# Splitting the transformed 3x3 convolution's matmuls into four column-tiled ones

## The chip, the cores and the metric

The kernel runs on one core of a Trainium2 chip. The metric is the device time of one execution in microseconds, the median of the runs shown. A core has TensorE (PE in the profile, with its weight loads as PEld), VectorE (DVE), ScalarE (ACT), GpSimd (POOL) and SyncE (SP), which here issues most of the DMAs. Matmul results land in PSUM; everything else that is worked on lies in SBUF.

## The reference

The input x has 8 images of 512 channels by 32 x 32 pixels, all float32. Two residual layers follow each other. Only the first one holds the code of this change.

```
x = x + L0(group_norm(x))
    t = silu(bn(conv1x1(x)));  ys = [t[:, :256], t[:, 256:]]
    for i in range(2):
        yi = ys[-1]
        z = silu(bn(conv3x3(yi, m_cv1_w[i])))      # 256 -> 256 channels   <- changed here
        z = attention(z, qkv_w[i], rw[i] + rh[i])   # 4 heads of 64, 1024 positions
        z = silu(bn(conv1x1(z, m_cv2_w[i])))
        ys.append(yi + z)
    silu(bn(conv1x1(concat(ys), cv2_w)))
x = x + L1(group_norm(x))
    depthwise 3x3, bn, relu, prune; conv1x1, bn, relu, prune
```

## The kernel before

The images are worked on one after the other, with channels on the 128 partitions and the 1024 pixels along the free dimension. The order of all work is written out by hand. Each piece of work is registered under a short name (`add("P", ...)`), and strings of names (`FIRST`, `HEAD`, `TAIL`, `LAST`) say in which order the pieces are issued: `P` is a call of `products`, `d` a step of the input transform, `Rc` and `R` the two steps that take a result back out of PSUM, `B`, `E` and `Ez` the rest of the back transform, `s`, `e`, `p` and `w` the steps of attention. A class `InOrder` (L95) ties every engine's instructions to that order; since it issues all of them, every line of the profile carries L105, and groups are told apart by the tiles that they write and read.

The 3x3 convolutions don't multiply pixel by pixel. `conv3` (L725) transforms the input rows along x (`along_rows`) and along y (`across_rows`) on VectorE into three pairs of planes j, each in one tile: `comps` (L741) names `kr`, `vt` and `qy`, which are free at this point, for j = 0, 1, 2. A tile holds four components c of 512 columns. In a component, 128 columns belong to each pair of output half i and input block k, in the order 2 * i + k. The weights were transformed in the same way at the start and stored in DRAM (`u_dram`); each call of `products` takes one tile of them, 128 x 2048, from a ring of five (`ring`, profile name `wring`), and `ring_load` fetches the next.

`products(j, m)` (L791) makes for one pair of planes j and one block m of 128 output channels all the products of transformed weights and transformed input: for each of four components c and two halves i, two matmuls of 128 input channels by 128 output channels by 128 columns, which add up over k in the same place of a PSUM tile. That tile, `ps_c3` (`ps_c` in the profile), is 128 x 1024 and comes from a pool of two, `ps_big`, that attention and the 1x1 convolutions use too. `rows_back` (L810) then copies one component to SBUF on ScalarE and adds and subtracts the four on VectorE into `mid`. The six calls of one convolution follow each other on TensorE with no other matmul between them; 8 images, 2 layers and 6 calls make 96 calls of 16 products each.

Attention holds the two halves of the array apart already: scores (`ps_s`) and values (`ps_av`) work on quarters, 64 rows by 64 columns. The sums of the softmax (`sums`, L1030, tile `ps_dn`) use 128 rows and 32 columns, four tiles side by side:

```python
for i in range(4):
    t = sm[m, i // 2]
    nc.tensor.matmul(
        dn[32 * i : 32 * (i + 1), :], ones, t[:, i % 2, :], start=True, stop=True
    )
```

Of the kernel before, what the change touches and what calls it, by code (L numbers as in the profile page):

```python
# [15 lines left out]
P = 128  # L16
# [4 lines left out]
HEADS, HD = 4, 64  # L21
# [104 lines left out]
def fast_kernel(  # L126
# [16 lines left out]
    nc = Engines(tc)  # L143
# [18 lines left out]
    def big_tile(name):  # L162
        return ps_big.tile([P, 2, 512], F32, tag="big", name=name)
# [121 lines left out]
    def flat(ps):  # L285
        return ps.rearrange("p n f -> p (n f)")
# [126 lines left out]
    def ring_load(n=1):  # L413
        for _ in range(n):
            if not sources:
                continue
            if holds and len(sources) <= holds[0]:
                waiting[0] += 1
                continue
            src = sources.pop(0)  # L420
            t = ringp.tile([P, 2048], F32, tag="ring", name="wring")
            o = t[:, : src[1]]
            if src[1] == 1024:
                o = o.rearrange("p (k o) -> p k o", o=P)
            nc.sync.dma_start(o, src[0])
            ring.append(t)
# [298 lines left out]
    def conv3(l):  # L725
# [17 lines left out]
        def component(j, c):  # L743
            return comps[j][:, c * 512 : (c + 1) * 512]
# [46 lines left out]
        def products(j, m):  # L791

            ps = banks[j, m] = big_tile("ps_c3")
            u = ring.pop(0).rearrange("p (i c k o) -> p i c k o", i=2, c=4, k=2)
            for c in (1, 2, 0, 3):
                for i in range(2):
                    at = place[c] * 256 + i * P
                    for k in range(2):
                        nc.tensor.matmul(
                            flat(ps)[:, at : at + P],  # L800
                            u[:, i, c, k, :],
                            component(j, c)[:, (2 * i + k) * P : (2 * i + k + 1) * P],
                            start=(k == 0),
                            stop=(k == 1),
                        )
            ring_load()

        inner_planes, outer_planes, ys = {}, {}, {}
# [60 lines left out]
        for j in range(3):  # L869
            add("d", *[lambda j=j, i=i: along_rows(j, i) for i in range(2)])  # L870
            add("d", *[lambda j=j, i=i: across_rows(j, i) for i in range(2)])
        add("P", *[lambda j=j, m=m: products(j, m) for j, m in jm])
        add("Rc", *[lambda j=j, m=m: rows_back(j, m, 0) for j, m in jm])
        add("R", *[lambda j=j, m=m: rows_back(j, m, 1) for j, m in jm])
# [1000 lines left out]
```

## Time and profile before

| | |
|---|---|
| time, median of 2 runs | 2595.19 us (2595.06 to 2595.32) |
| span of the profiled execution | 2593.6 us |
| around the span, against the median | 1.6 us |
| mean granted TensorE clock | 0.997 |
| instructions | 36377, of them 14806 matmuls and as many weight loads |
| PE, DVE, ACT busy | 2557.7, 2054.9, 1214.4 us |
| ps_c matmuls | 3 groups (kr, vt, qy) of 1024, 119.4, 117.0 and 117.0 us |

The page gives the busy time of each engine, then the span in 40 slices, the DMA queues, the chain of work that ended last, and the costliest groups of instructions. A row of a group reads: line, engine, operation, output<-inputs, rows*columns of the array for a matmul, shape, count, then busy time in us, mean ns of one instruction, and the idle time ahead of it with what ended it. The duration of a single matmul reaches from its start to the modelled end of its pass through the array, so that it is longer than the distance between two; the distance is busy time or elapsed time divided by the count. Rows of the order of time read: start in us, length in us, engine, operation, count.

### The profile page before, as it was taken

What the parts mean: (1) busy time and instruction counts of PE and PEld (TensorE: products, weight loads), DVE (VectorE), ACT (ScalarE), POOL (GpSimd) and SP (SyncE); (2) the same over time, 40 slices, a digit from 0 to 9 for tenths busy, and PEclk for the clock granted to TensorE, in tenths of its full rate; (3) what the DMA queues carried; (4) which work ended last, traced back from release to release, by engine and by line L of the source; (5) the groups of instructions that cost most, each with busy time, mean ns of one, the idle gap of its engine ahead of it and who ended that gap; (6) DMA issues with size and microseconds to landing.
All of it is one profiled execution on the core that took longest, in us unless ns stands there. A gap on an engine that the chain in (4) does not pass through costs nothing.

```text
span 2593.6 us, 36377 instructions
## 1 busy us (share of the span) xinstructions
PE 2557.7 (99%) x14806; PEld 1292.0 (50%) x14806; DVE 2054.9 (79%) x2954; ACT 1214.4 (47%) x1551; POOL 129.2 (5%) x99
## 2 busy tenths in 40 slices
PE   8999999999999999999999999999999999999997
PEld 5454463634636346463464635545355544645443
DVE  8887588877897877877778778787788877888657
ACT  3635446353463544635445444544445454363534
POOL 1000000000100000000000000000001000010000
PEclk9999999999999999999999999999999999999998
DMA  9445230522305214060140702306122151312300
GB/s 347 157 155 203 66 122 25 167 98 73 113 27 199 66 65 122 17 247 18 65 122 17 248 18 81 105 24 241 33 96 75 61 204 34 130 45 82 122 17 34
DMA packets 83791, 268.51 MB, mean 104 GB/s; under 512 B 7072, under 2 KB 37536, under 8 KB 69408
## 3 DMA queue, kind: packets, MB, share of 16 engines
q1 hardware_dynamic: 76032, 248.01, 27.2%
q0 software_dynamic: 4032, 14.68, 3.1%
q10 hardware_dynamic: 3552, 3.41, 0.4%
q8 instruction: 118, 1.93, 0.3%
q14 instruction: 57, 0.47, 0.1%
HBM read 212.34 MB, written 36.96 MB: 96 GB/s over the span
## 4 chain that ended last, share of the span: by engine, by line
PE 95%; DVE 3%; ACT 1%; issue 0%; DMA 0%; SPq 0%; DVEq 0%; ACTq 0%
PE ps_av L105 16%; PE ps_s L105 16%; PE ps_c L105 13%; PE ps_cv L105 12%; PE ps_qk L105 8%; PE ps_cv2q L105 8%; PE ps_q L105 7%; PE ps_v L105 4%; PE ps_y L105 4%; PE ps_m L105 4%; PE ps_dn L105 1%; ACT qy L105 1%; DVE sum L105 1%; DVE ht L105 1%; PE ps_pw L105 0%
## 5 line engine op out<-in xcount | busy, mean ns | idle before, releaser
L105 ACT ACTIVATE e<-ps_s 128x1024 f32<-128x1024 f32 x512 | 509.7, 1023 | 286.8 <-PE ps_s L105 265.6
L105 PE MATMUL ps_s<-qy,kr 64*64 64x512 f32 x4096 | 513.7, 592 | 1.4
L105 DVE TENSOR_TENSOR sum<-sum,e 128x1024 f32<-128x1024 f32 x384 | 475.2, 1238 | 39.2 <-ACT e L105 19.9
L105 PE MATMUL ps_av<-e,vt 64*64 64x512 f32 x4096 | 506.2, 590 | 0.0
L105 DVE SCALAR_TENSOR_TENSOR ht<-xn,v_sb,ht 128x961 f32<-128x961 f32 (+1 forms) x256 | 317.3, 1247 | 8.6 <-ACT ht L105 5.0
L105 PEld LDWEIGHTS ps_s<-qy,kr 64*64 64x64 f32 x4096 | 160.5, 132 | 289.0 <-issue 191.1
L105 PEld LDWEIGHTS ps_av<-e,vt 64*64 64x64 f32 x4096 | 165.4, 133 | 277.4 <-issue 266.0
L105 PE MATMUL ps_qk<-z,wring 128*128 128x512 f32 x512 | 231.1, 596 | 2.0 <-ACT z L105 1.3
L105 DVE TENSOR_TENSOR sum<-e 128x1024 f32<-128x1024 f32 x64 | 78.1, 1220 | 164.0 <-ACT e L105 162.6
L105 ACT COPY c<-ps_c 128x256 f32<-128x256 f32 x96 | 35.6, 371 | 259.4 <-PE ps_c L105 259.3
L105 PEld LDWEIGHTS ps_qk<-z,wring 128*128 128x128 f32 x512 | 95.6, 190 | 115.7 <-issue 101.5
L105 DVE RECIPROCAL r<-ps_dn 128x128 f32<-128x128 f32 x128 | 113.7, 925 | 11.2 <-PE ps_dn L105 9.0
L105 PE MATMUL ps_c<-vt,wring 128*128 128x128 f32 x1024 | 119.4, 276 | 2.3 <-DVE v L105 1.3
L105 PEld LDWEIGHTS ps_c<-kr,wring 128*128 128x128 f32 x1024 | 116.8, 192 | 8.0 <-issue 6.1
L105 PEld LDWEIGHTS ps_c<-vt,wring 128*128 128x128 f32 x1024 | 116.2, 192 | 4.3 <-ACT c L105 2.3
L105 PE MATMUL ps_c<-qy,wring 128*128 128x128 f32 x1024 | 117.0, 275 | 0.0
L105 PE MATMUL ps_c<-kr,wring 128*128 128x128 f32 x1024 | 117.0, 275 | 0.0
L105 PE MATMUL ps_cv<-pt,w_sb 128*128 128x512 f32 x256 | 116.7, 607 | 0.0
L105 PE MATMUL ps_v<-wring,z 128*128 128x256 f32 x512 | 115.9, 379 | 0.7 <-DVE kr L105 0.7
L105 PEld LDWEIGHTS ps_c<-qy,wring 128*128 128x128 f32 x1024 | 115.6, 192 | 0.0
L105 PE MATMUL ps_m<-z,wm_sb 128*128 128x512 f32 x256 | 112.5, 592 | 0.0
L105 PE MATMUL ps_y<-pt,w_sb 128*128 128x512 f32 x256 | 112.3, 592 | 0.0
(178 smaller groups left out, 3255.5 us busy)
## 6 DMA issues: line engine op xcount, KB each, us to landing
wring<-u SPq DMA_DIRECT2D x96, 1024.0 KB, 4.8
pt<-in_x SPq DMA_DIRECT2D x32, 512.0 KB, 9.4
rw<-r SPq DMA_DIRECT2D x64, 256.0 KB, 3.4
xt<-in_x SPq DMA_DIRECT2D x32, 512.0 KB, 7.5
out<-xt SPq DMA_DIRECT2D x32, 512.0 KB, 8.0
kr<-r POOLq DMA_DIRECT2D x28, 512.0 KB, 6.6
wring<-q SPq DMA_DIRECT2D x14, 896.0 KB, 4.6
wring<-in_wqkv SPq DMA_DIRECT2D x16, 768.0 KB, 4.4
```

Source lines behind the costliest of these rows:

```text
L105: made = method(*args, **kwargs)
```

## The change

The two halves of the 128 columns (n) are multiplied separately, and for each the two halves of the 128 output channels (o). `HD` is 64. Each matmul has still 128 rows, but 64 columns of weights and 64 moving columns, and it writes one half of the PSUM partitions, by which it sits on the left or on the right half of the array's columns. The sums over k are finished for the first half of the columns before the second is begun. Everything else stays.

```diff
             for c in (1, 2, 0, 3):
                 for i in range(2):
                     at = place[c] * 256 + i * P
-                    for k in range(2):
-                        nc.tensor.matmul(
-                            flat(ps)[:, at : at + P],
-                            u[:, i, c, k, :],
-                            component(j, c)[:, (2 * i + k) * P : (2 * i + k + 1) * P],
-                            start=(k == 0),
-                            stop=(k == 1),
-                        )
+                    for n in (0, HD):
+                        for k in range(2):
+                            from_ = (2 * i + k) * P + n
+                            for o in (0, HD):
+                                nc.tensor.matmul(
+                                    flat(ps)[o : o + HD, at + n : at + n + HD],
+                                    u[:, i, c, k, o : o + HD],
+                                    component(j, c)[:, from_ : from_ + HD],
+                                    start=(k == 0),
+                                    stop=(k == 1),
+                                )
             ring_load()
```

## The prediction

> **What bounds the kernel now.** I read the page's shares of busy time first, then the chain that ended last, then the groups of instructions, then the order of time around one convolution and one attention stage.
>
> ```profile
> PE 2557.7 (99%) x14806; PEld 1292.0 (50%) x14806; DVE 2054.9 (79%) x2954; ACT 1214.4 (47%) x1551; POOL 129.2 (5%) x99
> ...
> PE 95%; DVE 3%; ACT 1%; issue 0%; DMA 0%; SPq 0%; DVEq 0%; ACTq 0%
> ...
> L105 PE MATMUL ps_c<-vt,wring 128*128 128x128 f32 x1024 | 119.4, 276 | 2.3 <-DVE v L105 1.3
> L105 PEld LDWEIGHTS ps_c<-kr,wring 128*128 128x128 f32 x1024 | 116.8, 192 | 8.0 <-issue 6.1
> ```
>
> TensorE is busy for 99% of the span and holds 95% of the chain. Whatever lengthens a matmul stage lengthens the program; there is no large wait in which it could hide. The three ps_c matmul groups (kr, vt, qy) are what the change touches: 3 x 1024 records. Each product in the code leaves two loads and two matmuls in the trace (two passes), so these are 1536 products: 96 calls of `products` (8 images, 2 layers, 3 components, 2 output blocks), each with 16.
>
> The longest pieces of the chain, in order of time, then the window of the same piece (columns of the last line: stretch, its length, then busy time of PE, PEld, DVE, ACT, POOL, clock, DMA share, GB/s):
>
> ```profile
> 347.58 21.44 PE ps_c L105 x192
> ...
> 347.58:369.02 21.44, 21.44 (x193) 21.44 (x193) 20.46 (x46) 3.77 (x11) 0.00 (x0) 1.00 0.61 209
> ```
>
> Here six calls follow one another without a gap: 21.44 us / 192 matmuls = 111.7 ns each, and 3072 x 111.7 = 343.1 us, 13% of the span, which is the share that the chain gives ps_c. In this stretch the loads (PEld) are busy all the time too, unlike over the whole span (50%). So each step of 111.7 ns is bounded by both: 128 moving columns stream while the next 128 columns of weights load.
>
> How column tiles behave is shown by a stage that has them already, ps_dn (128 rows by 32 columns, four tiles), between two attention stages of 64 by 64 tiles:
>
> ```profile
> 120.66 1.04 PE L105 MATMUL ps_av<-e,vt 64*64 64x512 f32 x8
> 121.63 1.07 PE L105 MATMUL ps_dn<-sum,ones 128*32 128x512 f32 x8
> 122.63 1.09 PE L105 MATMUL ps_s<-qy,kr 64*64 64x512 f32 x8
> 123.54 1.04 PE L105 MATMUL ps_av<-e,vt 64*64 64x512 f32 x8
> ...
> 121.63 0.16 PEld L105 LDWEIGHTS ps_dn<-sum,ones 128*32 128x32 f32 x8 [0.81 <-issue]
> ...
> L105 PEld LDWEIGHTS ps_dn<-sum,ones x256: 106/108/110, 121.6 to 2479.7; 128*32 128x32 f32 x128
> L105 PEld LDWEIGHTS ps_s<-qy,kr x4096: 129/133/133, 89.2 to 2476.1; 64*64 64x64 f32 x196
> L105 PEld LDWEIGHTS ps_c<-kr,wring x1024: 186/192/192, 43.3 to 2383.6; 128*128 128x128 f32 x171
> ```
>
> To be seen: (1) eight ps_dn matmuls of 512 columns take 1.07 us, where eight in a row would take 8 x 0.43 = 3.4 us (a full-array 512-column matmul, ps_qk, costs 231.1 us / 512 = 0.45). So four column tiles of the same 128 rows run at once, in two rounds of 0.43 us. (2) Their eight loads are all done within 0.16 us: the loads of different column tiles run at once, and the second four run beneath the first four matmuls. (3) A load's median falls from 192 to 133 to 108 ns for 128, 64 and 32 columns, 0.75 to 0.92 ns a column on a fixed part. (4) A normal eight of this kind begins every 0.86 us; the ps_dn eight was late by 0.11 us, and ps_s came 1.00 us after it: a switch of tile shape costs something.
>
> [...] No group here shows a stream of 64-column matmuls.
>
> **The change, part by part.** Each product (128 input rows, 128 outputs, 128 columns, 2 passes of load and matmul) becomes four: two halves of the moving columns (n) by two halves of the outputs (o), on the left and right half of the array. The k loop now lies inside n, and o innermost, so neighbours in the program sit on different halves. Removed: 3072 loads of 128 columns and 3072 matmuls of 128. Added: 12,288 loads of 64 columns and 12,288 matmuls of 64. Multiplications are the same; loaded weight columns double in total, but two halves can load at once. No DMA, VectorE, ScalarE instruction or buffer is changed, and the waits on ring tile, component and psum tile stay at each call's start.
>
> *Step of one pair of tiles.* With both halves at once, a round is a left and a right matmul. In the trace's single starts, matmuls of 512 and 256 columns follow at 428.8 and 215.8 ns, 0.83 ns a column[...]. So the old step is 128 x 0.833 = 106.7 ns plus 5.0 fixed = 111.7. With the same fixed part, a step of 64 columns is an estimated 53.3 + 5.0 = 58.3 ns. Four rounds (n twice, passes twice) replace two steps: 4 x 58.3 = 233.2 against 2 x 111.7 = 223.4 ns, +9.8 ns a product; 1536 of them: +15.0 us. The gain from halves is exactly eaten by the doubled count, and what remains is the fixed part paid twice.
>
> Nothing in before shows this step, so I bound it. Below: streaming, 53.3 ns, plus the smaller fixed part of the 512-column steps (428.8 - 512 x 0.833 = 2.2): 55.5 ns, -1.4 ns a product, -2 us. Above: the halves do not overlap at all, 8 x 58.3 = 466 ns, +243 ns a product, +373 us. I take 58.3, as ps_dn shows the overlap.
>
> *Instructions.* A round now hands over 4 instructions in 58 ns, where it was 2 in 112. In the trace's single starts, the four loads and four matmuls of a ps_s round begin within 27 ns, about 3.4 ns each; between waits of PE's own sequencer, 8 instructions pass in 74 ns and 16 in 88, 1.75 ns more for each. So 14.6 ns each is inside what was seen, though only in bursts. PE's program was fetched in pieces of 256 instructions, about 1 us each; one call now uses such a piece in 3.7 us, so I cost fetching at nothing. If it were not hidden, 96 calls at about 1 us would add up to 96 us.
>
> *Switches.* The program's order keeps the six calls of a convolution together: 16 runs, each entered from and left to 128x128 products. Before, these had no switch. From single starts, a switch takes 95 ns from the end of streaming, after which the first load is exposed: 55 ns for 64 columns, 107 for 128. That is 0.15 in, 0.20 out: 16 x 0.35 = +5.6 us. Where TensorE waits anyway (37 steps of ps_c longer than usual sum to 5.7 us over the normal step) part of it, and of the longer calls, may hide: at most about 5 us, which I leave in the range.
>
> *Sum.* 2593.6 + 15.0 + 5.6 = 2614.2 us of span; 1.6 us lay around it in the profiled execution's time against the median of 2595.19, so 2615.8 us, +0.8%. About 2% is what a measurement of this kernel can tell from no change, so the forecast is "no difference".
>
> **Rivals.**
> 1. *Small steps cost more than their columns (slower).* Place: within each round, where the left half's and the right half's load and matmul are handed over in turn. If the second half starts 6.7 ns after the first (the distance of neighbours in a ps_s round) and the next round's left half must wait for it, and a load adds its own, a round is 53.3 + 2 x 6.7 = 66.7 ns: 266.8 a product, +43.4 ns, +66.7 us; with the switches 2667.5 us. It decides for "slower" from a round of 63.4 ns on ((51.9 - 5.6) us / 1536 / 4 = 7.5 over 55.85), only 5 ns above mine. For it:[...] no such stream in before. Against it: the ps_s rounds, where four tiles add 2.2 ns to 426.6 in all.
> 2. *The halves run one after the other.* 2595.2 + 373 + 5.6 = 2974 us.[...] Against it: ps_dn, whose four tiles share all rows.
> 3. *Nothing changes.* Round 55.5 ns and the switches hidden under waits: about 2595 us. For it: the load may have less fixed part when two run. Against it: PE waits little around ps_c. A gain over 2% is excluded by streaming: 4 x 53.3 = 213.3 ns is 10 ns under 223.4, 15.5 us at most.
>
> **How the numbers follow.** Forecast 0.60 (2603 to 2640 us), nothing changes 0.05, costlier steps 0.20 (2640 to 2720, of which some just inside 2%), one after the other 0.13, any gain 0.02. The range reaches from 2600 into the costlier steps, to 2700, and leaves out the serial case. Slower by over 2% (above 2647): 0.13 + about 0.20 = 0.33; faster 0.01; the rest 0.66.
>
> **What would show it.** Right: the piece of 21.44 us with 192 matmuls becomes one of about 384 x 58.3 = 22.4 us with 768, loads of 64 columns near 133 ns, left and right starting in pairs; all other groups keep their durations. About 25.6 us there means rival 1, about 45 rival 2. It would be wrong if that piece stays near 22 us and the time still grows, through gaps ahead of ps_c (fetching, switches).

## The result, and the profile after

| | before | after |
|---|---|---|
| time, median | 2595.19 us | 2635.72 us (2634.93 to 2636.51) |
| ratio | | 1.0157, 95% interval 1.0127 to 1.0186 |
| span of the profiled execution | 2593.6 us | 2633.1 us |
| matmuls in the profile | 14806 | 24022 |
| instruction packets of queue q8 | 118 | 190 |

The change costs 40 us, twice the forecast 20.6 us, and stays inside the 2% and the range. First the page of the kernel after: PE's busy share, the chain, the groups of ps_c.

```profile
PE 2580.6 (98%) x24022; PEld 1312.4 (50%) x24022; DVE 2058.6 (78%) x2954; ACT 1212.0 (46%) x1551; POOL 129.1 (5%) x99
...
PE 95%; DVE 2%; ACT 1%; DMA 1%; issue 1%; ACTq 0%; SPq 0%
...
L105 PE MATMUL ps_c<-qy,wring 128*64 128x64 f32 x4096 | 126.9, 224 | 9.9 <-issue 9.8
L105 PE MATMUL ps_c<-vt,wring 128*64 128x64 f32 x4096 | 124.9, 222 | 7.8 <-issue 7.3
L105 PEld LDWEIGHTS ps_c<-kr,wring 128*64 128x64 f32 x4096 | 121.0, 138 | 12.7 <-issue 6.7
```

The groups hold 4096 matmuls for 1024, and are busy for 5.5 to 9.9 us more each: kr 123.2 for 117.0 us, vt 124.9 for 119.4, qy 126.9 for 117.0 (in the table of before, 119.4 is the figure of vt). New is the idle time ahead of the matmuls of vt and qy, with the releaser "issue": time in which the engine waited for nothing that the profile shows. In before the matmul groups had 2.3 us or less, in after these two show 7.8 and 9.9. The loads of kr waited on "issue" in before already, 6.1 us, for 6.7 in after.

Next, the order of time of two convolutions of the first layer in the kernel after. The first is undisturbed, the second is not.

```profile
359.42 7.68 PE L105 MATMUL ps_c<-kr,wring 128*64 128x64 f32 x256
366.93 7.64 PE L105 MATMUL ps_c<-vt,wring 128*64 128x64 f32 x256
374.40 7.64 PE L105 MATMUL ps_c<-qy,wring 128*64 128x64 f32 x256
381.96 1.56 PE L105 MATMUL ps_y<-pt,w_sb 128*128 128x512 f32 x3
...
689.80 5.19 PE L105 MATMUL ps_c<-vt,wring 128*64 128x64 f32 x172
694.82 2.03 PE L105 MATMUL ps_c<-qy,wring 128*64 128x64 f32 x63
697.97 5.87 PE L105 MATMUL ps_c<-qy,wring 128*64 128x64 f32 x193 [1.12 <-issue]
```

And the piece of the chain that the prediction asked for:

```profile
359.49 22.55 PE ps_c L105 x768
```

To be seen: where nothing interferes, 768 matmuls take 22.55 us with the last one's way through the array; rounds of two start 58.3 ns apart. The prediction said 22.4 us. In the second convolution TensorE stops in the middle of a call, after 63 matmuls, for 1.12 us, and no other engine is the releaser.

The stops have one mark in common. I numbered TensorE's instructions in the order in which they started and looked up where each stop longer than 0.14 us from one matmul's start to the next falls. In the kernel after there are 25 such stops inside the ps_c runs. Two of them, 0.4 and 0.5 us in the first image, stand where before waits as well, at the first load of vt. The other 23, 0.09 to 3.35 us beyond a normal step and 21.5 us together, all lie at the same place, 193 or 194, counted modulo 256. Each ends 2.2 to 2.7 us after an instruction packet of 16,384 bytes began on queue q8. Such a packet holds 256 instructions: the change adds 9216 loads and 9216 matmuls to the trace, and 72 packets for these 18,432. I read this as TensorE out of program until the next piece was there. In the kernel before, no stop within ps_c lies there.

The longest stop, in the first image, was followed by more: during 3.4 us of the next piece of program the granted clock was 0.50, and these 256 instructions took 5.28 us, where 3.73 us is normal. Whether the stop brought the clock down is not shown.

### The profile page after: what moved, and what is told of

It reads as the page before. It is cut to its first block, busy times and chain, and to the rows that moved or that the text cites. A ratio compares the mean times of both kernels' runs of the same rounds, so it can differ in the third digit from the quotient of the medians.

```text
span 2633.1 us, 54791 instructions
## 1 busy us (share of the span) xinstructions
PE 2580.6 (98%) x24022; PEld 1312.4 (50%) x24022; DVE 2058.6 (78%) x2954; ACT 1212.0 (46%) x1551; POOL 129.1 (5%) x99
## 4 chain that ended last, share of the span: by engine, by line
PE 95%; DVE 2%; ACT 1%; DMA 1%; issue 1%; ACTq 0%; SPq 0%
PE ps_av L105 16%; PE ps_s L105 16%; PE ps_c L105 13%; PE ps_cv L105 12%; PE ps_qk L105 8%; PE ps_cv2q L105 8%; PE ps_q L105 6%; PE ps_v L105 4%; PE ps_m L105 4%; PE ps_y L105 4%; PE ps_dn L105 1%; ACT qy L105 1%; DVE ht L105 1%; PE ps_pw L105 0%; DMA s<-scomb 0%
## 5 line engine op out<-in xcount | busy, mean ns | idle before, releaser
L105 PEld LDWEIGHTS ps_qk<-z,wring 128*128 128x128 f32 x512 | 96.4, 190 | 111.7 <-issue 102.6
L105 PE MATMUL ps_c<-qy,wring 128*64 128x64 f32 x4096 | 126.9, 224 | 9.9 <-issue 9.8
L105 PE MATMUL ps_c<-vt,wring 128*64 128x64 f32 x4096 | 124.9, 222 | 7.8 <-issue 7.3
L105 PEld LDWEIGHTS ps_c<-qy,wring 128*64 128x64 f32 x4096 | 124.0, 139 | 11.4 <-issue 11.4
L105 PEld LDWEIGHTS ps_c<-kr,wring 128*64 128x64 f32 x4096 | 121.0, 138 | 12.7 <-issue 6.7
L105 PEld LDWEIGHTS ps_c<-vt,wring 128*64 128x64 f32 x4096 | 122.0, 138 | 9.5 <-issue 9.4
L105 PE MATMUL ps_c<-kr,wring 128*64 128x64 f32 x4096 | 123.2, 223 | 0.5 <-issue 0.5
```

Source lines behind the costliest of these rows:

```text
L105: made = method(*args, **kwargs)
```

## The experiments

**Theory:** rounds and switches cost what was priced, and the rest is TensorE waiting for its own instructions, 256 at a time. **Rivals:** waits for PSUM or weights; column tiles or small moving sizes that cost more than their columns.

**Output halves alone.** Two products for four, each with all 128 moving columns.

```diff
-                    for n in (0, HD):
-                        for k in range(2):
-                            from_ = (2 * i + k) * P + n
-                            for o in (0, HD):
...
-                                    flat(ps)[o : o + HD, at + n : at + n + HD],
...
-                                    component(j, c)[:, from_ : from_ + HD],
...
+                    for k in range(2):
+                        from_ = (2 * i + k) * P
+                        for o in range(0, P, HD):
...
+                                flat(ps)[o : o + HD, at : at + P],
...
+                                component(j, c)[:, from_ : from_ + P],
```

> Only the split of the 128 output channels is kept: 128 moving columns, 64 outputs on each half, 8 instructions of the program for a product where the change has 16. Theory (instruction supply): the extra 19 us beyond the priced rounds and switches are stalls in which TensorE's program is late, one piece of 256 instructions at a time; here a piece lasts 7 us, so no stall is left. A round streams 106.7 ns plus the small fixed part of a streaming-bound step, 2.2, so 108.9 ns against 111.7: 1536 x 2 x -2.8 = -8.6 us, switches +5.6: about 2592 us. Rival (waits for PSUM or weights): the calls are even shorter than in the change, so the stalls stay, about 2610 us. Rival (column tiles themselves cost more than their columns): over 2600 us, spread over all rounds.

Measured: 2593.7 us (2592.5 to 2597.39) against 2594.91 for before on the same chip, ratio 0.9997 (0.9988 to 1.0006): no difference. The chain of this kernel:

```profile
348.47 21.11 PE ps_c L105 x384
```

384 matmuls, two at a time, take 21.11 us, 110 ns a round, against 111.7 ns for a step before. That is 1 ns above the 108.9 expected from the 0.83 ns a column at which longer matmuls follow each other in before, so the loads of 64 columns (138 ns each in the kernel after, in pairs) add nothing to the step of two. Of the 0.33 us that a convolution gains in this piece, its two switches take back about 0.2: from the last matmul ahead of it to the second after it, the run takes 22.17 us for 22.30. No stop of more than 0.1 us lies at the 256 mark. Column tiles are not what costs.

**Output quarters.** The same loop with 32 in place of `HD`: as many instructions as the change, but no matmul with fewer than 128 columns.

> The 128 output channels in four quarters of 32, 128 moving columns: as many instructions as the change (16 a product) in rounds of four tiles, with no 64-column matmul in it. Theory (instruction supply): array time as with halves, 2 x 108.9 ns a product, but 256 instructions last only 3.5 us, so the stalls come back, 15 to 30 us: 2605 to 2622 us, with long gaps at one place in every piece of 256 instructions. Rival (waits for PSUM or weights): the same time as the halves, whatever it is. Rival (small moving size is what costs): no stall, about 2592 us.

Measured: 2640.54 us (2639.12 to 2641.95), ratio 1.0178 (1.0161 to 1.0195), 47 us above the halves, which do the same array work in the same streaming steps (256 matmuls of kr in 7.19 us here, 128 in 7.21 us there). It was 18.5 us more than the upper end of what I had expected. Its order of time in one convolution:

```profile
676.66 7.19 PE L105 MATMUL ps_c<-kr,wring 128*32 128x128 f32 x256
683.67 1.92 PE L105 MATMUL ps_c<-vt,wring 128*32 128x128 f32 x61
687.13 5.76 PE L105 MATMUL ps_c<-vt,wring 128*32 128x128 f32 x193 [1.54 <-issue]
...
695.93 5.65 PE L105 MATMUL ps_c<-qy,wring 128*32 128x128 f32 x196 [1.39 <-issue]
```

The first component's 256 matmuls take 7.19 us without a stop; then TensorE stops for 1.54 and for 1.39 us, with "issue" as the releaser. In the whole kernel 52 stops lie at the 256 mark, 44 to 47 us together, by what one takes as the normal distance between two matmuls of different rounds; that is about the difference to the halves. This pair of runs settles it: array work equal, instructions doubled, and the cost appears at the pieces' borders. That the quarters lose more than the change fits their pace, 256 instructions in 3.5 us for 3.7; it isn't shown by itself.

**Smaller weight loads.** The change, with a quarter of each transformed weight tile loaded and used; the other three quarters are left out.

```diff
-                    yield u_dram[l][i].rearrange("p a b c d -> p (a b c d)"), 2048
+                    yield u_dram[l][i].rearrange("p a b c d -> p (a b c d)")[:, :512], 512
...
-        nc.vector.tensor_scalar(sc12, sc[:, BN2 : BN2 + 4], -1.0 / 12.0, None, ALU.mult)
+        nc.vector.tensor_scalar(sc12, sc[:, BN2 : BN2 + 4], -1.0 / 1200.0, None, ALU.mult)
...
-            u = ring.pop(0).rearrange("p (i c k o) -> p i c k o", i=2, c=4, k=2)
+            u = ring.pop(0)[:, :512].rearrange("p (i k o) -> p i k o", i=2, k=2)
...
-                                    u[:, i, c, k, o : o + HD],
+                                    u[:, i, k, o : o + HD],
```

> The change with a quarter of each transformed weight tile loaded (256 KB for 1024 KB) and used for all four components; the convolution's output is scaled down by 100 so that the softmax stays finite. Left out: three quarters of the transformed weights. Instructions of TensorE are those of the change. Theory, with the supply delayed by the weight loads on the same DMA engines: most stalls inside ps_c go, about 2616 to 2620 us. Theory, with the supply slow by itself: they stay, about 2635 us. Rival (waits for PSUM): they stay too, 2635 us.

Measured: 2628.26 us (2625.15 to 2631.44), ratio 1.0132 (1.0115 to 1.0149), between the two. 21 stops are left at the 256 mark, 16.7 us for 21.5; a longest of 1.9 us for 3.3. So the weight loads lengthen the stops but don't make them: with a quarter of those bytes most of them stay. (Four executions against the change's two are few, but their ranges don't overlap.)

What sets a late piece apart can be read from the packets. In each of the two kernels 80 pieces of 256 instructions lie wholly within ps_c. I took for each the time from the border at which TensorE enters it to the start of the packet that brings the next one. In the kernel after it was 1.5 to 4.8 us for the 23 late pieces and at most 1.5 us for the others, but for one under the halved clock. From the packet's start to the first use of what it brings, no piece took less than 2.2 us, and 3.7 us for a piece less 2.2 is 1.5. So it is the packet's late start that makes the stop. With the smaller loads it is the same, 1.5 us or more for the 21 late pieces and at most 1.3 for the others. The late starts go together with busy DMA engines: where packets of other queues filled 90% or more of the 16 engines' time in the first 1.4 us after the border, 16 of 19 pieces were late, and 1 of 41 where they filled 60% or less. With the smaller loads these are 14 of 15 and 4 of 58. That the instruction packets wait behind this data is my guess from these counts: no run varied the traffic alone, so it is not shown.

**The first pair of calls alone.** The loop of the change where `j == 0`, the old one else.

> Only the two calls on the first pair of planes (j = 0) are split in four, the other four of each convolution stay whole: 512 products for 1536, two switches a convolution as before. Theory (instruction supply): 512 x 9.8 ns = 5.0 us and 5.6 us for switches, and few stalls, as two pieces of 256 instructions are mostly there when the run begins: 2605 to 2609 us. Rival (stalls belong to every call alike): a third of 19 us on top, 2612 us.

Measured: 2600.98 us (2600.17 to 2603.07), ratio 1.0024 (1.0015 to 1.0034), 4 us below the lower end of what was expected. Each undisturbed run of six calls is 0.67 us longer than before in the first layer, as priced (32 x 9.8 ns + 0.35 = 0.66), but only 0.24 us in the second, where TensorE had short waits before. Two stops at the 256 mark are left, both in the first image, 1.1 us together, not the third of 21.5 that "every call alike" would be. Two calls of 256 instructions pass mostly unharmed, six in a row do not.

**Column halves alone.** All 128 outputs, 64 moving columns, so that every load has 128 columns.

```diff
-                            for o in (0, HD):
-                                nc.tensor.matmul(
-                                    flat(ps)[o : o + HD, at + n : at + n + HD],
-                                    u[:, i, c, k, o : o + HD],
...
+                            nc.tensor.matmul(
+                                flat(ps)[:, at + n : at + n + HD],
+                                u[:, i, c, k, :],
```

> Only the split of the 128 moving columns is kept: all 128 outputs, 64 columns each. Theory (a step is the longer of streaming and loading, and the two halves of the array undo the doubled loads in the change): every step still loads 128 columns of weights, 111.7 ns, and there are twice as many: 1536 x 223.4 = +343 us, about 2938 us, with no switch and no late instructions (256 of them last 14 us). Rival (the step is bounded by streaming and instruction count, loads are hidden): rounds near 60 to 70 ns, 2595 to 2660 us.

Measured: 2930.4 us, ratio 1.1291 (1.1268 to 1.1313), 8 us under the sum. Its chain:

```profile
43.86 42.84 PE ps_c L105 x384
...
387.20 42.82 PE ps_c L105 x384
```

384 matmuls in 42.82 us are 111.5 ns each, as long as with twice the columns: the step goes with the 128 weight columns loaded, not with the moving ones. This is what the output halves pay back in the change: two loads of 64 columns at once (in the kernel after the second of a pair starts 7 ns behind the first, and each lasts 138 ns).

**The halves apart.** The change with the loop over o outermost, so that four products of the left half precede four of the right.

```diff
-                    for n in (0, HD):
-                        for k in range(2):
-                            from_ = (2 * i + k) * P + n
-                            for o in (0, HD):
+                    for o in (0, HD):
+                        for n in (0, HD):
+                            for k in range(2):
+                                from_ = (2 * i + k) * P + n
```

> The same instructions as the change, with the loop over the output halves outermost: the four products of the left half (16 instructions) stand in the program before the four of the right half. Theory ([...]neighbours in the program are not needed): rounds of 58.3 ns as in the change, and the same late pieces of 256: about 2635 us, 2625 to 2650. Rival (only neighbours overlap): the halves run one after the other but for the seams, 200 to 370 us more, and then no late pieces, since the instructions last twice as long.

Measured: 2697.64 us (2697.52 to 2700.62), ratio 1.0398 (1.038 to 1.0415). Neither expectation held. Its chain:

```profile
361.32 27.93 PE ps_c L105 x768
499.80 27.93 PE ps_c L105 x768
```

27.93 us for 48 groups of sixteen matmuls are 582 ns each: ten steps of 58 ns, where full overlap needs eight and none sixteen. The records don't name the half, but some loads are shorter, 133 ns for 138, as the first two of a run are in the kernel after, and I take them to mark where the other half begins. In the single starts of one group the right half's first load comes only once the left half is at its fifth matmul of eight, when five instructions of the left still wait. With seven of them waiting, one step earlier, it had not come. So in this group the load went ahead of five waiting instructions and not of seven, and neighbours on different halves matter: 582 ns for these sixteen matmuls, 8 x 58.3 = 466 in the change's order. And there is only one stop at the 256 mark outside the first image, of 0.2 us: with these longer steps a piece of 256 instructions lasts 4.65 us, and the same number of instructions is supplied in time.

## Why the prediction was right or wrong

*The step of one pair of tiles* was right: 58.3 ns predicted, 58.3 measured, and the piece of the chain 22.55 us for 22.4. The overlap of column tiles, read from ps_dn, held for 64-column tiles over all rows. The old step, put down to streaming and loading alike, was bounded by the load: 111.5 ns a step with half the moving columns, 110 with half the loaded ones. Rival 1, costlier small steps, and rival 2, one half after the other, fall with this number.

*Switches* were right. A run of six calls, from the last matmul ahead of it to the second after it, grew from 22.30 to 23.61 us where nothing interferes, +1.31; the sum said (15.0 + 5.6) / 16 = 1.29.

*Instructions* was the step that failed: "so I cost fetching at nothing". It measured 21.5 us, inside the 96 us that stood as the price if it were not hidden. I had shown that TensorE can accept instructions quickly in bursts, and took this and the length of a packet, about 1 us (in before 118 packets on q8, median 1.04 us), for a supply that keeps up with 3.7 us a piece. A burst says nothing of the time from one delivery to the next, which also holds the delay until the packet starts, up to 4.8 us, and at least 2.2 us from its start to the first use. Where two pieces in a row were late in the kernel after, their first matmuls are mostly 3.9 to 4.6 us apart, longer than the 3.7 us of a piece.

*Hiding* was sized about right (at most 5 us): in the second layer's seven later convolutions, waits of 0.42 us each are gone, 2.9 us.

The sixteen runs, each from the last matmul ahead of it to the second after it, grew from 364.5 to 403.9 us together, which is 39.4 of the 39.5 us that the span grew. The parts come to the same: 16 x 1.31 = 21.0, less 2.9, plus 21.5, is 39.6 us. That it fits so closely is partly chance, as the sum leaves out the other waits of the first image, in before and in after, and the halved clock. The forecast of "no difference" at the 2% bound was kept, but the time lies nearer to that bound than my 0.60 for 2603 to 2640 us suggests: two of three terms fit, and the third was left out. That it was kept with half of the cost missing is luck: it held because the stops came to 21.5 us and not to more than 33. The closing sentence of the prediction had named the sign, a piece that stays near 22 us while the time grows through gaps; only they lie inside ps_c, at the pieces' borders, and not ahead of it.

## What to carry to other kernels

Splitting a matmul into tiles of the same total work left the array's time nearly alone here as long as neighbours in the program sat on different tiles (21.11 us in two, 22.55 in four, for 21.44 of a convolution), but it multiplies instructions, and those have to be delivered. 256 instructions of TensorE in 4.65 us nearly always came in time (one stop outside the first image), and in 3.5 to 3.7 us they were late again and again (52 and 23 times), mostly while the DMA engines were busy with data (in the kernel after 16 of 19 late at 90% or more, 1 of 41 at 60% or less), so count the instructions per microsecond of a dense stretch as one counts its columns. Idle time with "issue" as its releaser in the middle of a run of equal matmuls, at distances in the program that are multiples of 256 instructions, was the sign: 23 of the 25 stops.

## What the runs showed of the hardware that I had not expected

TensorE's program came in packets of 16,384 bytes, 256 instructions each (72 packets for 18,432 instructions more). What a border between two of them costs depended on the pace: within ps_c there was no stop at one at before's 14 us a piece and none of more than 0.1 us at 7 us (output halves), but 23 of 21.5 us together at 3.7 us and 52 of 44 to 47 us at 3.5 us.

TensorE started work for another tile ahead of waiting instructions, but in the group that was looked at past five of them and not past seven: with eight matmuls of one half ahead of eight of the other, a group took 582 ns, ten steps of 58 ns instead of eight.
